# Attention values made for 256 pixels of each half in one job, with the column of ones in the weights

## The chip, the cores and the metric

The kernel runs on one core of a Trainium2 chip. The core has four compute engines, each with its own in-order queue: TensorE (PE in the profile, with its weight loads as PEld), VectorE (DVE), ScalarE (ACT) and GpSimd (POOL). SyncE (SP) issues most of the DMAs. Matrix products land in PSUM, everything else lives in SBUF. The metric is the device time of one execution in microseconds (us).

## The reference

The input `x` has 8 images of 192 channels and 64 x 64 pixels. Two layers follow each other, each with a residual sum and with a group normalisation `_gn` in front (32 groups of 6 channels). Cut to what matters:

```python
q = prelu(conv1x1(x, w1, b1), a1)        # 24 channels
k = prelu(conv1x1(x, w2, b2), a2)        # 24 channels
v = prelu(conv1x1(x, wa, ba), aa)        # 192 channels
score = softmax(einsum('bnc,bcm->bnm', q, k), axis=2)   # 4096 x 4096 per image
out = einsum('bnm,bmc->bnc', score, v)
...
x = x + attention(_gn(x))                # layer 0
x = x + density(_gn(x))                  # layer 1
```

The density layer sends every pixel minus and plus 0.5 through a small network for each channel (widths 1, 3, 3, 3, 1, with tanh gates) and takes the difference of two sigmoids.

## The kernel before

The 192 channels are three groups `g` of 64 partitions, and the 4096 pixels of an image are two halves `s` of 2048, so that 128 partitions hold 64 channels of either half. Everything is float32; each matrix product appears in the profile as two records.

**The stream.** Attention is a loop of 1024 steps: 8 images, 8 blocks of 512 query pixels (`NB`), 16 steps each (`STEPS`). A step puts on TensorE, in this order: the scores of the next step (`scores`, L786, 2 products into the PSUM tile `sc`), a row-maximum product for a block to come (`max_products`, L714, 2 products into `mx`, which VectorE reduces in L722), and the sums of this step (`attend`, L801, 8 products of 193 columns into one of the two tiles `turns`, named `b` in the profile). ScalarE takes the exponential of the scores (L790). The 193rd column of a values tile is 1, so the sums also give the softmax's denominator. `sc` and `mx` have one buffer each: the next scores wait for the exponential, and the next maximum product for the reduce.

**Jobs.** Whatever else needs PSUM while the stream runs is a job, which is a guest in the tile of `turns` that the running block doesn't use: keys and queries (`keys`, L626), values (`values`, L675), transposes of the maxima (L751) and of the output (L834), norms (L462, L477) and weights (L553, L558). `start_job` starts at most one per step, by rank, and only if enough PSUM halves are free and, where the job asks for `cols` of scratch, a scratch pair is. A job returns its parts as `(steps later, function, VectorE cost, ScalarE cost, TensorE credit)`. `run_due` adds the credit to what VectorE and ScalarE may spend on density work (`density_step`): units of small instructions, above all L1053 on VectorE, L1021, L1030, L1036 and L1046 on ScalarE. The whole order is thus written out when the kernel is built, step by step; the engines then run it in their queues' order.

**A values job** makes 128 pixels of both halves: 4 products (three channel groups and one with `one_row`, which adds the bias row) for each of two halves, the halves in the two tiles of 64 rows of the array, side by side. Then `prelu` evacuates: two relus on ScalarE (L602) from PSUM into a scratch pair, of x and of -x, and a merge on VectorE (L605) into the values tile. There are two scratch pairs, `pra` and `prb`, of 2 x 192 columns; `ready` says from which step each is free. A pair of 256-pixel input tiles `xi` thus needs two values jobs. The columns of ones are set once, by GpSimd (L590).

**The head.** The first image's keys and values and the maxima of its first blocks are made before the stream. There a loop takes one values job per turn from a list and one or two maximum products from another, into the tiles `sc_head` and `mx_head`, each reduced by L722. Values of the other seven images are made in the stream, during the image before.

**The tail.** After the last step, the density work that is left follows, with some of its sums on TensorE (L994).

`weights` scales the convolution weights by the norm for each image (`wa_sb` becomes `wf["v"]`) and makes the offset of the bias row (`wf["ba"]`, from `ba_row` and L558).

Of the kernel before, what the change touches and what calls it, by code (L numbers as in the profile page):

```python
# [9 lines left out]
F32 = mybir.dt.float32  # L10
AF = mybir.ActivationFunctionType
ALU = mybir.AluOpType
# [5 lines left out]
def kernel(  # L18
# [142 lines left out]
    for i in range(2):  # L161
# [3 lines left out]
        bb.append(w)  # L165
        w = const.tile([128, 1], F32, name=f"slope{i}")
        slope.append(w)
    wa_sb = const.tile([128, 3, C], F32, name="wa_sb")
    ba_row = const.tile([128, C], F32, name="ba_row")
    one_row = const.tile([128, 128], F32, name="one_row")  # L170
    vslope = const.tile([128, 1], F32, name="vslope")
    nslope = const.tile([128, 3], F32, name="nslope")
    for t in (*wr, ba_row, one_row):
        nc.vector.memset(t, 0.0)
    nc.vector.memset(one_row[0:1], 1.0)
    nc.vector.memset(one_row[R : R + 1], 1.0)

    for i in range(2):
        nc.vector.tensor_reduce(
# [24 lines left out]
    def spread():  # L204

        for i in range(2):
            for k in range(4):
                at = slice(32 * k, 32 * k + CR)
                p = slice(R * (k % 2), R * (k % 2) + R)
                nc.gpsimd.tensor_copy(wr[i][p, :, at], (s2 if k // 2 == i else s1)[p])  # L210
        for g in range(3):
            nc.gpsimd.tensor_copy(
                wa_sb[:, g, :].rearrange("p (h r) -> p h r", h=3),
                sa[:, g, :].rearrange("p (r h) -> p h r", h=3),
            )
        for s in range(2):
            p = slice(R * s, R * s + 1)
            nc.gpsimd.tensor_copy(
                ba_row[p].rearrange("p (h r) -> p h r", h=3),
                sb[p].rearrange("p (r h) -> p h r", h=3),  # L220
            )

# [131 lines left out]
    ]  # L354

    scratch = []
    for k in "ab":
        pair = []
        for i in range(2):
            u = work.tile([128, 2 * C], F32, tag=f"pr{k}{i}", name=f"pr{k}{i}")  # L360
            pair.append(u)
        scratch.append(pair)
    ready = [0, 0]


# [14 lines left out]
    def start_job(t):  # L380
        p = t % STEPS
        for n, (rank, make, hold, banks, cols) in enumerate(jobs):
            if stream[0] and (p < 3 or p + max(hold, 1) >= STEPS):
                continue
            rooms = [(pm, g) for pm, g in homes if sum(k <= t for k in g) >= banks]
            if not rooms:
                if rank < 2:
                    return
                continue
            k = [i for i in (1, 0) if ready[i] <= t and scratch[i][0].shape[1] >= cols]  # L390
            if cols and not k:
                continue
            del jobs[n]
            pm, guest = min(rooms, key=lambda r: max(r[1]))
            at_ = [i for i in range(2) if guest[i] <= t]
            for i in at_[:banks]:
                guest[i] = t + hold + 1
            if cols:
                ready[k[0]] = t + 2
            spot[0] = next(n for n, k in enumerate(turns + others) if k is pm), at_[0]  # L400
            parts = make(pm if banks == 2 else pm[:, at_[0], :], scratch[k[0]] if cols else None)
            for i, fn, cost, act, pe in parts:
                at(t + i, fn, cost, act, pe)
            return
# [130 lines left out]
    def weights(b, then):  # L535
# [26 lines left out]

        def offsets():
            pf = cell["pf"]
            for i in range(2):
                d = wf["b", i, b] = fold.tile([128, 2], F32, tag=f"b{i}", name=f"b{i}_{b}")
                cell["read"](nc.vector.tensor_tensor(
                    d[:, 0:1], bb[i], pf[:, 2 * i : 2 * i + 1], ALU.subtract
                ))
                nc.vector.tensor_scalar(d[:, 1:2], d[:, 0:1], -1.0, None, ALU.mult)  # L570
            d = wf["ba", b] = fold.tile([128, C], F32, tag="ba", name=f"ba_{b}")
            cell["read"](nc.vector.tensor_tensor(d, ba_row, pf[:, 4 : 4 + C], ALU.subtract))
            then()

        at(now[0] + 1, scale, 0.3, 2.0)
# [11 lines left out]
    vtiles = []  # L587
    for i in range(NC + 2):
        v = vpool.tile([128, 2, 4, C + 1], F32, tag=f"v{i}", name=f"v{i}")
        nc.gpsimd.memset(v[:, :, :, C : C + 1], 1.0)  # L590
        vtiles.append(v)
    qt = {}

# [66 lines left out]
            )  # L660
        made.add(("q", b, c))

    def values(b, d, k, what, done):

        t = xi[what, b, d]
        c, h = divmod(d, 2)

        def make(pv, u):
            if (b, c) not in vt:
                vt[b, c] = vtiles.pop(0)  # L670
            v = vt[b, c][:, :, 2 * h + k, 0:C]
            for g in range(4):
                for s in range(2):
                    p = slice(R * s, R * s + R)
                    nc.tensor.matmul(  # L675
                        pv[:, s, 0:C],
                        lhsT=t[p, g, k * 128 : k * 128 + 128] if g < 3 else one_row[p],
                        rhs=wf["v", b][p, g, :] if g < 3 else wf["ba", b][p],
                        start=g == 0, stop=g == 3,
                    )  # L680
            done()
            first, last = prelu(
                ("v", b, d, k), v, pv[:, :, 0:C], None, nslope[:, 2:3],
                [x[:, 0 : 2 * C].rearrange("p (s n) -> p s n", s=2) for x in u],
            )
# [106 lines left out]
    def attend(t):  # L792
# [5 lines left out]
        assert ("v", b, 2 * ORDER[p // 4] + p % 4 // 2, p % 2) in made  # L798
        for s in range(2):
            for j in range(4):  # L800
                nc.tensor.matmul(  # L801
# [496 lines left out]

    def use(b, d, what, t, k, v, after=0):

        left = [k + 2 * v]

        def done():
            left[0] -= 1
# [7 lines left out]
        def work():  # L1312
            if k:
                keys(b, d, what, done)
            if v:
                for i in range(2):
                    values(b, d, i, what, done)

        at(t, lambda: request("xi", begin))

# [63 lines left out]
    ahead.extend([place(m)[1:]] for m in range(STEPS, LEAD))  # L1384
    while todo or ahead:
        if todo:
            make, d, *k = todo.pop(0)
            make(0, d, *k, "first", lambda: None)
# [88 lines left out]
```

## Time and profile before

| What | Value |
|---|---|
| Median of 3 runs | 4778.19 us (4777.09 to 4778.64) |
| Profiled execution | 4772.86 us |
| Its span | 4771.1 us |
| PE busy | 4654.9 us, 98% |
| DVE busy | 4162.7 us, 87% |
| ACT busy | 3198.0 us, 67% |
| POOL busy | 865.9 us, 18% |
| L801 PE, sums of the stream, x16384 | 2955.0 us |
| L675 PE, values from `xi`, x1344, and the bias row, x512 | 139.5 us and 62.9 us |
| L602 ACT, relus of 384 columns, x144 and x112 | 62.5 us and 48.6 us |
| L605 DVE, merges of 384 columns, x72 and x56 | 43.9 us and 34.5 us |

Busy time is the union of an engine's instructions, and its share is an average over head, stream and tail. Products are pipelined, so the distance between two starts says more than a duration. In lines of the timeline the columns are the start, the time until the last of the merged instructions ends (both in us), the engine, the line of the kernel, the operation, output and inputs, shapes, the count, and in brackets the idle time before and what ended it. In lines by stretch, the columns are the stretch, its length, then busy time and instruction count of PE, PEld, DVE, ACT and POOL, the granted TensorE clock, the DMA share and GB/s.

### The profile page before, as it was taken

The page shows a single profiled execution, that of the slowest core. Times are in us where ns is not written, and L with a number is a line of the kernel's source. Part 1 is how long each engine was busy: PE and PEld are TensorE (multiplying, and loading weights), DVE is VectorE, ACT ScalarE, POOL GpSimd, SP SyncE. Part 2 cuts the span into 40 slices and gives each one's busy share as a digit, 9 for nine tenths or more (in the row PEclk, how much of TensorE's full clock was granted, in tenths as well). Part 3 has the DMA queues.
Part 4 walks back from the last instruction along what each step waited for, and adds up shares of the span by engine and source line. Part 5 has one row for each costly group of instructions (what it writes and reads, how often), then busy time and mean ns, then how long its engine had stood idle before and what let it go on. Part 6 is the DMA issues. An engine that isn't in the chain of part 4 may idle for free.

```text
span 4771.1 us, 69026 instructions
## 1 busy us (share of the span) xinstructions
PE 4654.9 (98%) x28432; PEld 3442.5 (72%) x28432; DVE 4162.7 (87%) x4289; ACT 3198.0 (67%) x3665; POOL 865.9 (18%) x842
## 2 busy tenths in 40 slices
PE   7999999999999999999999999999999999999796
PEld 5777777777777777777777777777777777777332
DVE  5433359999999999999999999999999999998888
ACT  2332246767677777876777767777777777778675
POOL 0000001222222212221312322132222122132000
PEclk9999999999999999999999999999999999999898
DMA  2101020111100111110110111101111101000000
GB/s 59 41 18 29 18 48 14 35 28 30 46 24 25 37 39 34 27 41 12 36 46 26 30 40 36 32 16 36 36 38 33 31 16 27 10 6 22 9 14 14
DMA packets 109328, 138.60 MB, mean 29 GB/s; under 512 B 17106, under 2 KB 82132, under 8 KB 109012
## 3 DMA queue, kind: packets, MB, share of 16 engines
q1 hardware_dynamic: 107776, 133.81, 11.5%
q8 instruction: 223, 3.65, 0.3%
q14 instruction: 93, 0.76, 0.1%
q10 hardware_dynamic: 1236, 0.37, 0.0%
HBM read 100.58 MB, written 29.36 MB: 27 GB/s over the span
## 4 chain that ended last, share of the span: by engine, by line
PE 95%; ACT 2%; DVE 2%; DMA 0%; issue 0%; POOL 0%; ACTq 0%; SPq 0%; DVEq 0%; POOLq 0%
PE b L801 60%; PE sc L786 22%; PE b L675 4%; PE b L994 2%; PE b L626 2%; PE mx L714 1%; PE sc_tail L994 1%; PE mx_tail L994 1%; DVE d L1053 1%; PE b L834 1%; PE b L751 1%; ACT d L1046 0%; ACT d L1021 0%; ACT e L790 0%; ACT d L1002 0%
## 5 line engine op out<-in xcount | busy, mean ns | idle before, releaser
L801 PEld LDWEIGHTS b<-v,e 128*128 128x128 f32 x16384 | 2651.1, 190 | 776.0 <-issue 764.6
L801 PE MATMUL b<-v,e 128*128 128x193 f32 x16384 | 2955.0, 334 | 0.0
L790 ACT ACTIVATE e<-sc 128x1024 f32<-128x1024 f32 x1024 | 1045.4, 1021 | 1320.1 <-PE mx L714 1282.6
L722 DVE TENSOR_REDUCE rm<-mx 128x1 f32<-128x1024 f32 x1002 | 1223.0, 1221 | 477.5 <-PE mx L714 471.1
L786 PE MATMUL sc<-q,k 25*128 25x512 f32 x4096 | 1154.2, 640 | 4.1 <-ACT e L790 3.8
L714 PE MATMUL mx<-k,q 24*128 24x512 f32 x4008 | 1129.4, 640 | 0.0
L1053 DVE SCALAR_TENSOR_TENSOR d<-d,lc,d 128x1024 f32<-128x1024 f32 x756 | 974.0, 1298 | 16.7 <-ACT d L1030 4.8
L1053 DVE SCALAR_TENSOR_TENSOR d<-d,wsp,d 128x1024 f32<-128x1024 f32 x684 | 876.2, 1284 | 50.6 <-ACT d L1046 42.5
L1174 POOL MEMSET pause<- 128x1 f32 x408 | 40.3, 99 | 3590.1 <-DVE d L1053 3590.1
L1053 DVE SCALAR_TENSOR_TENSOR d<-d,tf,d 128x1024 f32<-128x1024 f32 x540 | 685.7, 1287 | 0.4 <-ACT d L1036 0.4
L1036 ACT ACTIVATE d<-d 128x1024 f32<-128x1024 f32 x540 | 566.8, 1052 | 34.4 <-DVE d L1053 34.1
L786 PEld LDWEIGHTS sc<-q,k 25*128 25x128 f32 x4096 | 306.2, 183 | 229.6 <-issue 188.9
L1046 ACT ACTIVATE d<-d,cb,wsp 128x1024 f32<-128x1024 f32 x348 | 429.2, 1235 | 0.6
L1021 ACT ACTIVATE d<-xc,bn,wn 128x1024 f32<-128x1024 f32 x288 | 353.4, 1234 | 0.8 <-issue 0.8
L1084 POOL TENSOR_TENSOR d<-d,d 128x512 f32<-128x512 f32 x168 | 335.8, 1999 | 36.9 <-ACT d L1078 35.7
L1030 ACT ACTIVATE d<-xc,bn,wn 128x1024 f32<-128x1024 f32 x252 | 311.3, 1235 | 0.0
L714 PEld LDWEIGHTS mx<-k,q 24*128 24x128 f32 x4008 | 299.6, 183 | 9.1 <-DVE rm L722 8.2
L1209 POOL TENSOR_TENSOR d<-d,d 128x512 f32<-128x512 f32 x80 | 170.2, 2127 | 0.0
L1221 POOL TENSOR_TENSOR d<-d,d 128x512 f32<-128x512 f32 x80 | 170.1, 2126 | 0.5 <-issue 0.5
L1229 POOL TENSOR_TENSOR d<-d,d 128x512 f32<-128x512 f32 x80 | 159.4, 1992 | 1.7
L675 PE MATMUL b<-wv,xi 64*128 64x192 f32 x1344 | 139.5, 340 | 0.0
L675 PEld LDWEIGHTS b<-wv,xi 64*128 64x128 f32 x1344 | 106.5, 186 | 25.4 <-issue 23.6
(155 smaller groups left out, 2309.1 us busy)
## 6 DMA issues: line engine op xcount, KB each, us to landing
xi<-in_x_dram SPq DMA_DIRECT2D x280, 192.0 KB, 3.7
xc<-in_x_dram SPq DMA_DIRECT2D x64, 384.0 KB, 7.0
out_dram<-xc SPq DMA_DIRECT2D x94, 256.0 KB, 3.2
q<-qd SPq DMA_DIRECT2D x128, 128.0 KB, 2.7
k<-kq SPq DMA_DIRECT2D x64, 64.0 KB, 1.9
qd<-kq SPq DMA_DIRECT2D x64, 64.0 KB, 2.1
d<-in_x_dram SPq DMA_DIRECT2D x16, 192.0 KB, 4.1
out_dram<-xc SPq DMA_DIRECT2D x4, 128.0 KB
```

Of the source, the lines that this page charges most:

```text
L675: nc.tensor.matmul(pv[:, s, 0:C], lhsT=t[p, g, k * 128 : k * 128 + 128] if g < 3 else one_row[p], rhs=wf["v", b][p, g, :] if g < 3 else wf ...
L714: nc.tensor.matmul(sc[:, s, :], lhsT=tile_of(qt[b, n // 2], n, j)[r], rhs=kt[b][r, u : u + F], start=True, stop=True,)
L722: nc.vector.tensor_reduce(out=rowmax[b, n][:, j, k : k + 1], in_=sc, axis=AX.XY, op=ALU.max)
L786: nc.tensor.matmul(sc[:, s, :], lhsT=kt[b][r, k : k + 128], rhs=qt[b, n // 2][r, :, u : u + 256], start=True, stop=True,)
L790: return lambda: nc.scalar.activation(e, sc, AF.Exp)
L801: nc.tensor.matmul(a[:, j, 0 : C + 1], lhsT=e[:, s, j * 128 : j * 128 + 128], rhs=v[:, s, p % 4, :], start=p == 0 and s == 0 and j % 2 == ...
L1021: nc.scalar.activation(self.buf[k], self.src(), AF.Tanh, bias=bn[:, s, g, 0, i : i + 1], scale=wn[:, g, 0, i : i + 1],)
L1030: nc.scalar.activation(self.buf[k], self.src(), AF.Identity, bias=bn[:, s, g, 1, i : i + 1], scale=wn[:, g, 1, i : i + 1],)
L1036: nc.scalar.activation(self.buf[k], self.buf["l", k[1], k[2]], AF.Tanh)
L1046: nc.scalar.activation(self.buf[k], self.buf["l", n - 1, 0], AF.Identity, bias=offset, scale=wsp[:, g, w : w + 1],)
L1053: nc.vector.scalar_tensor_tensor(dst, src, factor, dst, ALU.mult, ALU.add)
L1084: return nc.gpsimd.tensor_tensor(z[:, n], z[:, n], dst[:, n], ALU.add)
```

## The change

One values job now makes 256 pixels of each half: both groups of 128 pixels, one after the other, into columns 0 to 192 and 193 to 385 of the same two PSUM banks. The evacuation is two relus of 772 columns and one merge of 772. Its scratch is both pairs together, which are now one pair of tiles of 772 columns; keys use one half of it, as before. Such a job starts only when both halves are free, and holds both for two steps. Its parts carry a credit of 2.75 for TensorE, 1.9 for ScalarE and 0.95 for VectorE, where each of the two jobs had 1.4, 1.1 and 0.62. The weights get a 193rd column of zeros and the bias row a 193rd element of one, so that the products give the column of ones, and the GpSimd memsets of it go away.

```diff
-    wa_sb = const.tile([128, 3, C], F32, name="wa_sb")
-    ba_row = const.tile([128, C], F32, name="ba_row")
+    wa_sb = const.tile([128, 3, C + 1], F32, name="wa_sb")
+    ba_row = const.tile([128, C + 1], F32, name="ba_row")
...
+    nc.vector.memset(wa_sb[:, :, C : C + 1], 0.0)
+    for k in (0, R):
+        nc.vector.memset(one_row[k : k + 1], 1.0)
+        nc.vector.memset(ba_row[k : k + 1, C : C + 1], 1.0)
...
-    for k in "ab":
-        pair = []
-        for i in range(2):
-            u = work.tile([128, 2 * C], F32, tag=f"pr{k}{i}", name=f"pr{k}{i}")
-            pair.append(u)
-        scratch.append(pair)
+    for i in range(2):
+        u = work.tile([128, 4 * C + 4], F32, tag=f"pr{i}", name=f"pr{i}")
+        scratch.append(u)
...
-            k = [i for i in (1, 0) if ready[i] <= t and scratch[i][0].shape[1] >= cols]
-            if cols and not k:
+            k = [i for i in (1, 0) if ready[i] <= t]
+            wide = cols > 2 * C
+            if cols and len(k) < 1 + wide:
                 continue
...
-            if cols:
+            u = None
+            if wide:
+                ready[:] = t + 2, t + 2
+                u = scratch
+            elif cols:
                 ready[k[0]] = t + 2
+                u = [x[:, 2 * C * k[0] : 2 * C * (k[0] + 1)] for x in scratch]
...
-                    pf[:, 4 : 4 + C], lhsT=cell["mb"][p], rhs=wf["v", b][p, g, :],
+                    pf[:, 4 : 5 + C], lhsT=cell["mb"][p], rhs=wf["v", b][p, g, :],
...
-        nc.gpsimd.memset(v[:, :, :, C : C + 1], 1.0)
...
-            v = vt[b, c][:, :, 2 * h + k, 0:C]
-            for g in range(4):
-                for s in range(2):
-                    p = slice(R * s, R * s + R)
-                    nc.tensor.matmul(
-                        pv[:, s, 0:C],
-                        ...
+            v = vt[b, c][:, :, 2 * h : 2 * h + 2, :].rearrange("p s k n -> p s (k n)")
+            for k in range(2):
+                for g in range(4):
+                    for s in range(2):
+                        p = slice(R * s, R * s + R)
+                        nc.tensor.matmul(
+                            pv[:, s, k * (C + 1) : (k + 1) * (C + 1)],
+                            ...
...
-                (0, lambda: None, 0.0, 0.0, 1.4), (1, first, 0.0, 1.1, 0.0),
-                (2, last, 0.62, 0.0, 0.0),
+                (0, lambda: None, 0.0, 0.0, 2.75), (1, first, 0.0, 1.9, 0.0),
+                (2, last, 0.95, 0.0, 0.0),
...
-        job(make, *((0, 1) if what == "v" else (k, 3)), 2, 2 * C)
+        job(make, *((0, 1) if what == "v" else (1, 3)), 2, 4 * C + 4)
...
-    todo += [(values, 2 * c + h, k) for c in ORDER for h in range(2) for k in range(2)]
+    todo += [(values, 2 * c + h) for c in ORDER for h in range(2)]
```

More of the change, by code (lines that the diff above doesn't have):

```diff
@@ L174 @@
         nc.vector.memset(t, 0.0)
-    nc.vector.memset(one_row[0:1], 1.0)
-    nc.vector.memset(one_row[R : R + 1], 1.0)
+    nc.vector.memset(wa_sb[:, :, C : C + 1], 0.0)
+    for k in (0, R):
+        nc.vector.memset(one_row[k : k + 1], 1.0)
+        nc.vector.memset(ba_row[k : k + 1, C : C + 1], 1.0)
     for i in range(2):
@@ L212, in spread @@
             nc.gpsimd.tensor_copy(
-                wa_sb[:, g, :].rearrange("p (h r) -> p h r", h=3),
+                wa_sb[:, g, 0:C].rearrange("p (h r) -> p h r", h=3),
                 sa[:, g, :].rearrange("p (r h) -> p h r", h=3),
@@ L218, in spread @@
             nc.gpsimd.tensor_copy(
-                ba_row[p].rearrange("p (h r) -> p h r", h=3),
+                ba_row[p, 0:C].rearrange("p (h r) -> p h r", h=3),
                 sb[p].rearrange("p (r h) -> p h r", h=3),
@@ L397, in start_job @@
                 guest[i] = t + hold + 1
-            if cols:
+            u = None
[3 more added lines that the diff above has]
+            elif cols:
                 ready[k[0]] = t + 2
+                u = [x[:, 2 * C * k[0] : 2 * C * (k[0] + 1)] for x in scratch]
             spot[0] = next(n for n, k in enumerate(turns + others) if k is pm), at_[0]
-            parts = make(pm if banks == 2 else pm[:, at_[0], :], scratch[k[0]] if cols else None)
+            parts = make(pm if banks == 2 else pm[:, at_[0], :], u)
             for i, fn, cost, act, pe in parts:
@@ L570, in offsets @@
                 nc.vector.tensor_scalar(d[:, 1:2], d[:, 0:1], -1.0, None, ALU.mult)
-            d = wf["ba", b] = fold.tile([128, C], F32, tag="ba", name=f"ba_{b}")
-            cell["read"](nc.vector.tensor_tensor(d, ba_row, pf[:, 4 : 4 + C], ALU.subtract))
+            d = wf["ba", b] = fold.tile([128, C + 1], F32, tag="ba", name=f"ba_{b}")
+            cell["read"](nc.vector.tensor_tensor(d, ba_row, pf[:, 4 : 5 + C], ALU.subtract))
             then()
@@ L661, in queries, with values @@
         made.add(("q", b, c))
-    def values(b, d, k, what, done):
+    def values(b, d, what, done):
         t = xi[what, b, d]
@@ L670, in make @@
                 vt[b, c] = vtiles.pop(0)
-            v = vt[b, c][:, :, 2 * h + k, 0:C]
-            for g in range(4):
-                for s in range(2):
-                    p = slice(R * s, R * s + R)
-                    nc.tensor.matmul(
-                        pv[:, s, 0:C],
[L677 to L680, printed above, removed]
+            v = vt[b, c][:, :, 2 * h : 2 * h + 2, :].rearrange("p s k n -> p s (k n)")
[5 more added lines that the diff above has]
+                            pv[:, s, k * (C + 1) : (k + 1) * (C + 1)],
+                            lhsT=t[p, g, k * 128 : k * 128 + 128] if g < 3 else one_row[p],
+                            rhs=wf["v", b][p, g, :] if g < 3 else wf["ba", b][p],
+                            start=g == 0, stop=g == 3,
+                        )
             done()
             first, last = prelu(
-                ("v", b, d, k), v, pv[:, :, 0:C], None, nslope[:, 2:3],
-                [x[:, 0 : 2 * C].rearrange("p (s n) -> p s n", s=2) for x in u],
+                ("v", b, d), v, pv[:, :, 0 : 2 * C + 2], None, nslope[:, 2:3],
+                [x.rearrange("p (s n) -> p s n", s=2) for x in u],
             )
             return [
-                (0, lambda: None, 0.0, 0.0, 1.4), (1, first, 0.0, 1.1, 0.0),
-                (2, last, 0.62, 0.0, 0.0),
+                (0, lambda: None, 0.0, 0.0, 2.75), (1, first, 0.0, 1.9, 0.0),
+                (2, last, 0.95, 0.0, 0.0),
             ]
-        job(make, *((0, 1) if what == "v" else (k, 3)), 2, 2 * C)
+        job(make, *((0, 1) if what == "v" else (1, 3)), 2, 4 * C + 4)
     rowmax = {}
@@ L797, in attend @@
         v = vt[b, ORDER[p // 4]]
-        assert ("v", b, 2 * ORDER[p // 4] + p % 4 // 2, p % 2) in made
+        assert ("v", b, 2 * ORDER[p // 4] + p % 4 // 2) in made
         for s in range(2):
@@ L1299, in use @@
     def use(b, d, what, t, k, v, after=0):
-        left = [k + 2 * v]
+        left = [k + v]
         def done():
@@ L1315, in work @@
             if v:
-                for i in range(2):
-                    values(b, d, i, what, done)
+                values(b, d, what, done)
         at(t, lambda: request("xi", begin))
@@ L1386 @@
         if todo:
-            make, d, *k = todo.pop(0)
-            make(0, d, *k, "first", lambda: None)
+            make, d = todo.pop(0)
+            make(0, d, "first", lambda: None)
         pair = list(zip(others, ahead.popleft() if ahead else ()))
```

## The prediction

> **What bounds the kernel now.** The first view read is the page: engine shares, then the chain that ended last.
>
> ```profile
> span 4771.1 us, 69026 instructions
> PE 4654.9 (98%) x28432; PEld 3442.5 (72%) x28432; DVE 4162.7 (87%) x4289; ACT 3198.0 (67%) x3665; POOL 865.9 (18%) x842
> PE 95%; ACT 2%; DVE 2%; DMA 0%; issue 0%; POOL 0%; ACTq 0%; SPq 0%; DVEq 0%; POOLq 0%
> ```
>
> TensorE is busy nearly always, and the chain runs through it for 95% of the span. An average hides stages, so the second view is busy time by stretch: head, stream, tail.
>
> ```profile
> 45.00:95.00 50.00, 46.37 (x363) 28.30 (x364) 37.12 (x45) 17.52 (x37) 0.00 (x0) 1.00 0.20 47
> 95.00:4420.00 4325.00, 4323.17 (x27383) 3280.49 (x27381) 3813.61 (x3913) 2939.92 (x3383) 849.93 (x805) 1.00 0.12 29
> 4420.00:4771.00 351.00, 266.38 (x620) 117.59 (x618) 295.10 (x275) 231.40 (x227) 10.66 (x11) 0.90 0.05 12
> ```
>
> In the stream (1024 steps from 94 to 4420 us) TensorE leaves 2 us of 4325 idle, VectorE is busy for 88% and ScalarE for 68%. There, time is what TensorE's queue holds. In the head and the tail it is not alone. The third view is TensorE's timeline over three steps.
>
> ```profile
> 603.30 0.70 PE L786 MATMUL sc<-q,k 25*128 25x512 f32 x2
> 604.38 2.88 PE L801 MATMUL b<-v,e 128*128 128x193 f32 x16
> 607.19 1.25 PE L675 MATMUL b<-wv,xi 64*128 64x192 f32 x12
> 608.26 0.49 PE L675 MATMUL b<-ba,one_row 64*128 64x192 f32 x4
> 608.69 0.70 PE L786 MATMUL sc<-q,k 25*128 25x512 f32 x2
> ```
>
> A values job stands alone between an attention block and the next scores and takes 608.69 - 607.19 = 1.50 us. Over the whole timeline, 693 plain steps have a median of 3.882 us and the 112 steps with a values job one of 5.382, none more than 1 ns from it: the job is paid in full, and none of it is hidden. The fourth view is the same timeline at the end of the head.
>
> ```profile
> 87.12 1.25 PE L675 MATMUL b<-wv,d 64*128 64x192 f32 x12
> 88.20 0.49 PE L675 MATMUL b<-ba,one_row 64*128 64x192 f32 x4
> 88.53 1.14 PE L675 MATMUL b<-wv,d 64*128 64x192 f32 x12
> 89.50 0.49 PE L675 MATMUL b<-ba,one_row 64*128 64x192 f32 x4
> 89.92 1.13 PE L786 MATMUL sc<-q,k 25*128 25x512 f32 x4
> 93.30 0.70 PE L786 MATMUL sc<-q,k 25*128 25x512 f32 x2 [2.25 <-ACT e L790]
> ```
>
> Two values jobs back to back take 89.92 - 87.12 = 2.80 us, not 3.00: going from the full array to two halves of 64 rows and back costs about 0.2 us, and here it is paid once for two jobs.
>
> **The stream: one change of array shape less per pair.** A wide job holds the same 32 TensorE records (16 products) as two narrow ones. By the rows it costs 2.80 us plus one column in 192 (0.5% of 2 x 1.30 us, 0.013): 2.81. Instead of 2 x 1.50 that is 0.187 less. Seven images make their values in the stream, 8 wide jobs each, and the built program has all 56 in steps of their own: 56 x 0.187 = **-10.5 us**.
>
> **ScalarE and VectorE.** Start to start, a relu of 384 columns takes 0.371 us on ScalarE and an exponential of 1024 takes 0.921, so one of 772 lies near 0.704; two replace four: 1.41 for 1.48 us. The merge on VectorE takes 0.526 at 384 columns, and L1053 takes 1.196 at 1024, so 772 lie near 0.93, for 1.05. Over 64 pairs that is 5 us of ScalarE and 8 us of VectorE, both with idle time in the stream: worth nothing directly. Cover gone, it would be 8 us. The Trainium skill (Perfetto Trace Analysis, Optimizing Scalar/DVE Operations) gives about 60 ns of overhead per VectorE operation; by that figure alone 64 merges fewer would be an estimated 4 us. The same section says that where these engines aren't saturated but cause bubbles on others, breaking instructions up may finish work sooner, which speaks against this change; by that rule the bubbles of the next part should grow.
>
> **The head: the order changes.** A wide job needs both scratch halves, so it may start only every second turn of the head's loop; narrow jobs alternated. In the built program's order a round of row maxima (one tile in `sc_head`, one in `mx_head`) formerly had a values job behind nearly every round. Now rounds stand in pairs with nothing between: R1 R2 W R3 R4 W R5 W R6 R7 W R8, transposes, S9 W S10 S11 W S12 S13 W S14 W, then the first scores (R round, S single tile, W wide job). A second tile in the same PSUM tile must wait for the reduce of the first:
>
> ```profile
> 46.55 1.22 DVE L722 TENSOR_REDUCE rm<-sc_head 128x1 f32<-128x1024 f32 x1
> 47.69 1.22 DVE L722 TENSOR_REDUCE rm<-mx_head 128x1 f32<-128x1024 f32 x1
> 48.82 0.48 DVE L605 SCALAR_TENSOR_TENSOR kq<-prb,nslope,prb 128x256 f32<-128x256 f32 x1
> ```
>
> Reduces follow each other by 1.14 us; a tile's matmuls came 1.27 after the start of the reduce they waited for (47.69 to 48.96); a reduce starts 1.18 after its matmuls (59.28 to 60.46); a tile alone takes TensorE 1.06, a round side by side 1.07. So two rounds in a row take 1.18 + 1.14 + 1.27 + 1.06 = 4.65 us, where two rounds with cover take 2.14; two single tiles 1.18 + 1.27 + 1.06 = 3.51. R8 to S9 takes 2.31 (second reduce) + 1.14 + 0.52 (72.19 to 72.71) + 0.56 (transposes) + 1.06 = 5.59. R2 ends 2.33 after 47.69, at 50.02. From there: 8 W x 2.81 = 22.48, two double rounds 9.30, R5 1.07, R8 to S9 5.59, two double singles 7.02, S14 1.06: 46.52. The first scores start at 96.54, not 89.92: **+6.6**. Behind them ScalarE evacuates the last job before it loads the table for the exponential: two relus of 0.81 and 0.70 instead of 0.49 and 0.37, so about **+0.6**. The scratch is single now, but each relu finds the merge before it done, except the last (0.1). Bounds for the head: +4, if half the lost cover is filled, and +9.
>
> **Stalls in the stream.** Plain steps exceed their median by 29.1 us in all, 5.0 of it in three steps (94, 1846 and 3488 us) in whose stretches the granted clock is 0.76. The other 24 come nearly all when a reduce or an exponential is late, about 2.4 of it per image in steps 12 to 17, where norm work and new density units meet. The planner gives a wide job 2.75 of credit at once and moves VectorE's density work by steps. I summed VectorE's work between each reduce and the next in both programs' order (rows' start-to-start times), against the step on TensorE with 1.6 us of grace for the reduce: surplus 7.3 us before, 8.6 after, all but 0.7 of it in steps 15 to 17 and near the end of the last image. So +1.3; the ledger sees only 7.3 of the 24, and scaled up it would be +4.3. I take **+2**, between -4 and +5.
>
> **Tail, start and stores.** TensorE's order in the tail is the same. On VectorE one L1053 (1.2 us), which ran at 4430.78 while L1250 waited for ScalarE, now stands behind L1251, ahead of the last residual and statistics that the final norm waits for: **+1.2** (-2 to +4, since the units after it are also reordered). Three small memsets more on VectorE (about 0.2 us) lie under its 9.4 us wait for x; six on GpSimd are gone from a stretch where it waits for weights; the 193rd column of the folded weights and bias costs some ns eight times. Nothing.
>
> **Sum.** -10.5 + 7.2 + 2 + 1.2 = -0.1. The profiled execution took 4772.86 us (span 4771.1 and 1.8 around it), 5.3 less than the median of the runs, 4778.19; the difference is applied to the latter: 4778.1, say 4778.
>
> **The rivals.** *Faster*: the head's pairs of rounds are covered better than I worked out (+4) and the stalls shrink by 4, since ScalarE and VectorE have 13 us less to do: -10.5 + 4 - 4 + 1.2 = -9.3, and with a tail unharmed -10.5: about 4768. For it: the steps are paid to the nanosecond. Against: the order of the head is fixed and its tiles do wait. *Slower*: the late reduce. The merge of 0.93 us in one piece stands ahead of reduces, and the credit of 2.75 lets three L1053 (3.6 us) stand beside it; 1.14 + 0.93 + 3.6 = 5.7 against 3.88 + 1.6 = 5.5. At 0.2 us for each of 56 jobs this costs 11: 4789. It decides once such a pile-up meets most of the jobs; the ledger finds it at few. *No saving inside the wide job*: the second half pays again, because it starts a new accumulation in the same bank: +10.4, 4788. Against it: the back-to-back row, though there the second job writes another tile.
>
> **Numbers.** No change (within 0.2%, 9.6 us, about what a measurement of this kernel can tell from no change): 0.62, own range 4769 to 4787. Faster 0.18. Slower 0.20, of which 0.12 for the late reduce and 0.08 for no saving. The range 4767 to 4790 takes in both other cases' centres and leaves out their far halves.
>
> **What would show it.** Right: a values step of 3.88 + 2.81 = 6.69 us; first attention block near 101.6, not 94.4 us; the stream from there some 8 us shorter; the tail about a microsecond longer. Wrong: a values step of 6.88; the first block before 98 us; excess of plain steps over 40 or under 15 us.

## The result, and the profile after

The changed kernel takes 4796.05 us (median of 5 runs, 4792.53 to 4797.34) against 4777.09 us for the one before (4772.67 to 4778.64): a ratio of 1.0044, with an interval of [1.0033, 1.0055]. It is slower by 0.4%, and outside the predicted range, which ended at 4790. The profiled execution after took 4796.05 us, with a span of 4794.3 us, 23.2 us longer than before (the medians are 19.0 apart; the execution profiled before was 4.2 us under its median). First the page, its lines for the span, the busy time and the chain that ended last (the changed kernel's lines are numbered 6 higher where it matters: values L681, maxima L720 and L728, scores L792, exponential L796, sums L807, density merge L1059):

```profile
span 4794.3 us, 68761 instructions
PE 4657.6 (97%) x28432; PEld 3452.8 (72%) x28432; DVE 4155.3 (87%) x4228; ACT 3192.3 (67%) x3537; POOL 857.1 (18%) x836
PE 91%; DVE 4%; ACT 3%; issue 1%; POOL 0%; DMA 0%; SPq 0%; ACTq 0%; DVEq 0%; POOLq 0%
```

VectorE and ScalarE have a little less to do, as worked out (7.4 and 5.7 us). But the chain now leaves TensorE for 9% of the span instead of 5%, and TensorE is busy 2.7 us longer for the same number of products. The busy time by stretch (head, stream, tail) says where:

```profile
45.00:114.00 69.00, 57.20 (x368) 36.69 (x366) 35.85 (x36) 16.13 (x22) 0.00 (x0) 0.83 0.17 39
114.00:4438.00 4324.00, 4315.55 (x27386) 3282.51 (x27384) 3804.92 (x3857) 2936.55 (x3271) 840.60 (x805) 1.00 0.12 29
4438.00:4794.00 356.00, 267.14 (x622) 118.34 (x618) 297.73 (x275) 231.30 (x227) 11.45 (x11) 0.90 0.05 12
```

The head ends at 114 us, not 94, and its granted clock is 0.83 where it was 1.00. The stream idles for 8.5 us of TensorE where it idled for 2. The tail is 5 us longer. From TensorE's timeline, to the first and from the last attention block:

| us, profiled execution | before | after | difference | predicted |
|---|---|---|---|---|
| first product (22.2 to 24.1 in the 14 executions below) | 22.85 | 24.07 | +1.2 | 0 |
| from there to the first attention block | 71.5 | 90.0 | +18.5 | +7.2 |
| stream, 112 or 56 values jobs | 168.0 | 158.0 | -10.0 | -10.5 |
| stream, what plain steps exceed 3.882 by, and small rests | 29.1 | 37.7 | +8.6 | +2 |
| tail | 350.8 | 355.7 | +4.9 | +1.2 |

The row of the jobs is 112 x 1.500 and 56 x 2.822: the median of the steps with a job, 5.382 and 6.704, less 3.882. One of them in TensorE's timeline, in image 4:

```profile
2537.07 2.88 PE L807 MATMUL b<-v,e 128*128 128x193 f32 x16
2539.88 1.25 PE L681 MATMUL b<-wv,xi 64*128 64x193 f32 x12
...
2542.70 0.70 PE L792 MATMUL sc<-q,k 25*128 25x512 f32 x2
```

A wide job takes 2542.70 - 2539.88 = 2.82 us, as predicted (2.81). So the job does what it should; the loss lies in the head and in the stalls. The head's timeline, first the products that waited:

```profile
49.44 1.13 PE L720 MATMUL sc_head<-k,q 24*128 24x512 f32 x4 [0.61 <-DVE rm L728]
...
58.57 1.48 PE L720 MATMUL sc_head<-k,q 24*128 24x512 f32 x4 [1.31 <-DVE rm L728]
...
72.99 1.13 PE L720 MATMUL sc_head<-k,q 24*128 24x512 f32 x4 [1.31 <-DVE rm L728]
...
82.10 0.63 PE L757 MATMUL b<-ident,negmax 128*128 128x128 f32 x4 [2.96 <-DVE negmax L751]
...
92.25 1.13 PE L720 MATMUL sc_head<-k,q 24*128 24x512 f32 x4 [1.33 <-DVE rm L728]
...
100.26 1.13 PE L720 MATMUL sc_head<-k,q 24*128 24x512 f32 x4 [1.33 <-DVE rm L728]
...
112.04 1.22 PE L792 MATMUL sc<-q,k 25*128 25x512 f32 x2 [2.90 <-ACT e L796]
```

The brackets are the idle time: 8.85 us before the six products of the maxima and transposes, where the kernel before had 0.25 and 1.07, and 2.90 before the second scores, where it had 2.25. The kernel before:

```profile
50.34 1.25 PE L675 MATMUL b<-wv,d 64*128 64x192 f32 x12 [0.25 <-ACT prb L602]
...
72.71 0.63 PE L751 MATMUL b<-ident,negmax 128*128 128x128 f32 x4 [1.07 <-DVE negmax L745]
```

That is 8.2 us more of waits; less 8 x 0.18 for the wide jobs, the order cost 6.7, against 7.2 predicted. The other 11.8 us of the head have another cause. Two wide jobs of this head, and a pair of rounds, from the timeline after:

```profile
61.71 2.30 PE L681 MATMUL b<-wv,d 64*128 64x193 f32 x12
...
66.64 0.70 PE L720 MATMUL sc_head<-k,q 24*128 24x512 f32 x2
...
70.53 0.70 PE L720 MATMUL sc_head<-k,q 24*128 24x512 f32 x2
...
75.18 1.25 PE L681 MATMUL b<-wv,d 64*128 64x193 f32 x12
...
97.80 1.13 PE L720 MATMUL sc_head<-k,q 24*128 24x512 f32 x4
...
101.31 1.25 PE L681 MATMUL b<-wv,d 64*128 64x193 f32 x12
...
104.14 1.13 PE L720 MATMUL sc_head<-k,q 24*128 24x512 f32 x4
```

The job from 61.71 takes 4.93 us, the one from 101.31 takes 2.83, for the same products. From 59.2 to 66.0 us the granted clock is 0.50, from 101.3 to 104.2 it is 1.00. Where it is full, the other pieces also came as worked out: the two rounds from 70.53 take 4.65 us, the two single tiles from 97.80 take 3.51. The trace has five stretches of half clock that begin in this head, from 52.4, 59.2, 83.1, 93.4 and 110.4 us, of 3.4 or 6.8 us, 27.2 us in all, of which 24.1 lie before the first attention block; the kernel before has none there. The eight wide jobs take 30.65 us instead of 8 x 2.81 = 22.48.

### The profile page after: what moved, and what is told of

Its sections match the earlier page's. It is cut to its first block, busy times and chain, and to the rows that moved or that the text cites. A ratio compares the mean times of both kernels' runs of the same rounds, so it can differ in the third digit from the quotient of the medians.

```text
span 4794.3 us, 68761 instructions
## 1 busy us (share of the span) xinstructions
PE 4657.6 (97%) x28432; PEld 3452.8 (72%) x28432; DVE 4155.3 (87%) x4228; ACT 3192.3 (67%) x3537; POOL 857.1 (18%) x836
## 4 chain that ended last, share of the span: by engine, by line
PE 91%; DVE 4%; ACT 3%; issue 1%; POOL 0%; DMA 0%; SPq 0%; ACTq 0%; DVEq 0%; POOLq 0%
PE b L807 57%; PE sc L792 21%; PE b L681 4%; DVE d L1059 3%; PE b L1000 2%; PE b L631 2%; PE mx L720 1%; PE mx_tail L1000 1%; PE sc_tail L1000 1%; PE b L840 1%; ACT d L1052 1%; PE b L757 1%; ACT d L1027 1%; ACT e L796 1%; DVE rm L728 1%
## 5 line engine op out<-in xcount | busy, mean ns | idle before, releaser
L807 PEld LDWEIGHTS b<-v,e 128*128 128x128 f32 x16384 | 2651.1, 190 | 776.7 <-issue 770.6
L807 PE MATMUL b<-v,e 128*128 128x193 f32 x16384 | 2954.9, 334 | 0.0
L796 ACT ACTIVATE e<-sc 128x1024 f32<-128x1024 f32 x1024 | 1044.7, 1020 | 1312.4 <-PE mx L720 1269.6
L728 DVE TENSOR_REDUCE rm<-mx 128x1 f32<-128x1024 f32 x1002 | 1223.7, 1221 | 485.6 <-PE mx L720 475.9
L792 PE MATMUL sc<-q,k 25*128 25x512 f32 x4096 | 1155.1, 640 | 11.3 <-ACT e L796 11.0
L720 PE MATMUL mx<-k,q 24*128 24x512 f32 x4008 | 1130.3, 640 | 0.0
L1059 DVE SCALAR_TENSOR_TENSOR d<-d,lc,d 128x1024 f32<-128x1024 f32 x756 | 971.6, 1295 | 16.5 <-ACT d L1036 4.8
L1059 DVE SCALAR_TENSOR_TENSOR d<-d,wsp,d 128x1024 f32<-128x1024 f32 x684 | 879.4, 1288 | 52.6 <-ACT d L1052 44.7
L1059 DVE SCALAR_TENSOR_TENSOR d<-d,tf,d 128x1024 f32<-128x1024 f32 x540 | 688.0, 1296 | 0.4 <-ACT d L1042 0.4
L1180 POOL MEMSET pause<- 128x1 f32 x408 | 39.9, 98 | 3603.4 <-DVE d L1059 3603.4
L792 PEld LDWEIGHTS sc<-q,k 25*128 25x128 f32 x4096 | 306.4, 183 | 237.9 <-issue 182.1
L720 PEld LDWEIGHTS mx<-k,q 24*128 24x128 f32 x4008 | 299.9, 183 | 11.1 <-DVE rm L728 10.1
L681 PE MATMUL b<-wv,xi 64*128 64x193 f32 x1344 | 134.7, 332 | 0.0
L607 ACT ACTIVATE pr<-b 128x772 f32<-128x772 f32 x128 | 97.0, 814 | 48.3 <-PE b L681 45.4
```

Of the source, the lines that this page charges most:

```text
L681: nc.tensor.matmul(pv[:, s, k * (C + 1) : (k + 1) * (C + 1)], lhsT=t[p, g, k * 128 : k * 128 + 128] if g < 3 else one_row[p], rhs=wf["v", ...
L720: nc.tensor.matmul(sc[:, s, :], lhsT=tile_of(qt[b, n // 2], n, j)[r], rhs=kt[b][r, u : u + F], start=True, stop=True,)
L728: nc.vector.tensor_reduce(out=rowmax[b, n][:, j, k : k + 1], in_=sc, axis=AX.XY, op=ALU.max)
L792: nc.tensor.matmul(sc[:, s, :], lhsT=kt[b][r, k : k + 128], rhs=qt[b, n // 2][r, :, u : u + 256], start=True, stop=True,)
L796: return lambda: nc.scalar.activation(e, sc, AF.Exp)
L807: nc.tensor.matmul(a[:, j, 0 : C + 1], lhsT=e[:, s, j * 128 : j * 128 + 128], rhs=v[:, s, p % 4, :], start=p == 0 and s == 0 and j % 2 == ...
```

## The experiments

Theories, after the result: the head is the order's idle time plus the half clock that the idle time brings; in the stream either the large pieces (two relus and a merge of 772 columns) hold up exponentials and reduces, or the credit, given once for two jobs, moves density work into full steps. What came out, with the profiled execution's head (first product to first attention block), half clock in it, stream and tail, the excess of the plain steps, and that excess without the steps that half clock touches:

| Kernel | median us (runs) | ratio to before | head | half clock | stream | excess | without half clock | tail |
| --- | --- | --- | --- | --- | --- | --- | --- | --- |
| before | (see above) | 1 | 71.5 | 0 | 4325.9 | 29.1 | 24.2 | 350.8 |
| after | 4796.05 (5) | 1.0044 [1.0033, 1.0055] | 90.0 | 24.1 | 4324.5 | 37.7 | 32.9 | 355.7 |
| narrow_head | 4779.64 (10) | 1.0013 [1.0003, 1.0023] | 74.0 | 5.5 | 4328.1 | 40.5 | 34.1 | 354.6 |
| narrow_stream | 4792.58 (5) | 1.0036 [1.0023, 1.0049] | 89.4 | 23.9 | 4327.1 | 29.2 | 24.2 | 347.9 |
| filled | 4786.18 (10) | 1.0024 [1.0015, 1.0034] | 83.2 | 9.6 | 4324.9 | 37.4 | 32.9 | 354.3 |
| credit | 4801.20 (4) | 1.0056 [1.0041, 1.0071] | 89.0 | 20.5 | 4327.8 | 40.1 | 34.4 | 360.0 |
| narrow_c1 | 4767.23 (1) | one run | 71.2 | 0.1 | 4320.9 | 23.4 | 19.3 | 350.5 |
| narrow_c2 | 4770.65 (1) | one run | 71.9 | 1.1 | 4325.2 | 27.7 | 22.4 | 348.0 |
| wide_c2 | 4780.14 (10) | 1.0008 [0.9999, 1.0018] | 72.1 | 1.3 | 4327.9 | 39.9 | 31.9 | 354.6 |
| split | 4783.44 (1) | one run | 72.2 | 1.7 | 4329.6 | 40.7 | 35.7 | 355.9 |
| spread | 4771.12 (10) | 0.9992 [0.9983, 1.0002] | 71.7 | 0 | 4321.8 | 35.0 | 31.6 | 350.0 |
| spread_c1 | 4765.56 (10) | 0.9982 [0.9973, 0.9992] | 72.2 | 2.4 | 4318.9 | 32.1 | 28.2 | 350.4 |
| narrow_c1_timed | 4770.62 (10) | 0.9992 [0.9983, 1.0002] | 74.3 | 5.2 | 4323.3 | 25.2 | 19.3 | 350.1 |
| narrow_lump | 4795.46 (1) | one run | 71.4 | 0 | 4350.3 | 52.0 | 44.0 | 348.0 |

The kernel before had a median of 4774.06 beside the first four experiments, 4775.30 beside the next four and 4774.02 beside the last four. "Loss" below is what steps of a typical one of the images 3 to 6 (images and steps counted from 0) run over their median, counting those over 60 ns and without half-clock steps: 3.9 us per image before, 6.1 after. Of the edits only the lines that matter are shown.

### The two halves of the change, apart

**narrow_head**: the head makes its values in narrow jobs, in the order of before; the stream is that of after.

```diff
-    def values(b, d, what, done):
+    def values(b, d, what, done, ks=(0, 1)):
...
-    todo += [(values, 2 * c + h) for c in ORDER for h in range(2)]
+    todo += [(values, 2 * c + h, (k,)) for c in ORDER for h in range(2) for k in range(2)]
```

> The head makes the first image's values in 16 narrow jobs as the kernel before did; the stream keeps the 56 wide jobs of the changed kernel, in the same order of instructions. Theory 'head': the changed kernel lost some 18 us because pairs of maximum rounds stand uncovered in the head and TensorE, idle between them, was granted half its clock; here the first attention block starts at 94 to 96 us instead of 114, the granted clock in the head is 1.0, and the total is 4778 to 4783 us. Theory 'late reduce': the loss lies in the stream, where a wide evacuation delays the reduces; here the head gains at most 7 us (its order alone) and the total stays above 4788 us. Either way the stream from the first to the last attention block should take 4324.5 us as in the changed kernel.

**narrow_stream**: the reverse; the stream makes narrow jobs, each with 1.4, 1.1 and 0.62, and its order is that of before.

```diff
-                values(b, d, what, done)
+                for i in range(2):
+                    values(b, d, what, done, (i,))
```

> The other half alone: 8 wide jobs in the head, 112 narrow jobs in the stream, whose order of instructions is that of the kernel before. Theory 'head': the first attention block starts at 112 to 115 us with stretches of half clock, the stream takes 4326 us as before, and the total is 4793 to 4798 us. Theory 'late reduce': the total is below 4786 us, since the stream no longer holds a wide job.

With the narrow head the head is back at 74.0 us and the time at 1.0013; with the narrow stream the excess is back at 29.2 and the tail at 347.9, but the head stays at 89.4 and the time at 1.0036. So the head carries most of the loss, and the stalls and the longer tail come with the wide jobs of the stream. Theory 'head' holds, with small misses: narrow_head's clock was 0.95 and its first attention block came at 96.5 us, narrow_stream's at 111.6. Narrow_head's stream was 3.6 us longer than after's although the order is the same: the steps that half clock touches cost 7.2 us in it and 4.9 in after, and two late reduces of image 5 (steps 36 and 38), 1.2 together, are not in after's execution.

### The clock in the head

**filled**: after, with 38 products of 126 columns that nobody reads, put ahead of the waiting products (2, 6, 6, 12, 6 and 6).

```diff
+    def busy(n):
+        for _ in range(n):
+            nc.tensor.matmul(
+                pm[:, 0, 386:512], lhsT=ident, rhs=ident[:, 0:126], start=True, stop=True
+            )
...
+        if pair and lone[0]:
+            busy(2 if pair[0][1] == (0, 1, 0) else 6)
```

> The changed kernel with its order, but in the six places of the head where TensorE waited for a reduce or for the transposes' input, products of 126 columns of the identity are put in front of the waiting product (2, 6, 6, 12, 6 and 6 of them, each about 0.22 us at full clock), into PSUM columns that nothing reads. They do no useful work and should end before the wait does. Theory 'idle halves the clock': the granted clock stays near 1.0 in the head, every wide job takes 2.8 us there instead of up to 5.4, the first attention block starts at 102 to 104 us instead of 114, and the total is 4784 to 4788 us. Theory 'load halves the clock' (the half clock follows the dense 64-row products, not the gaps): the clock still falls, the first block starts at 114 us or later, and the total is 4796 us or more.

The heads by stretch, of filled and of narrow_head (after's line stands above):

```profile
45.00:105.00 60.00, 56.70 (x432) 38.61 (x432) 35.85 (x36) 15.29 (x20) 0.00 (x0) 0.92 0.16 38
```

```profile
45.00:96.00 51.00, 47.42 (x360) 29.08 (x356) 36.69 (x44) 17.05 (x36) 0.00 (x0) 0.95 0.18 45
```

With more work in it the head is 6.8 us shorter, and its half clock went from 24.1 to 9.6 us. Each product of a filler takes the place of idle time, so what was gained is the clock's. The expectation of a clock near 1.00 was a miss: two stretches of 6.8 us stayed, one of them from 102.7 us, in the 2.90 us of waiting for the first exponential, which were not filled; what keeps the other, from 48.1, is open. The first attention block came at 105.5 us, not 102 to 104. The table prices the half clock: take half of it off each head, and the four with wide jobs in the head (after, narrow_stream, filled, credit) are left with 77.4 to 78.8 us, the ten others with 71.0 to 71.7. So a microsecond of half clock in the head costs about half of one, and the order about 7, as the waits gave.

### Credit or large pieces

**credit**: after, with larger costs for the wide job.

```diff
-                (0, lambda: None, 0.0, 0.0, 2.75), (1, first, 0.0, 1.9, 0.0),
-                (2, last, 0.95, 0.0, 0.0),
+                (0, lambda: None, 0.0, 0.0, 2.8), (1, first, 0.0, 2.2, 0.0),
+                (2, last, 1.24, 0.0, 0.0),
```

> The changed kernel with other numbers for the planner alone: a wide job carries 2.8 of credit for TensorE, 2.2 for ScalarE and 1.24 for VectorE, the sums of two narrow jobs, in place of 2.75, 1.9 and 0.95. No instruction is added or taken away; where density work stands in the stream changes. Theory 'chance placement': the excess of plain steps over their median (37.7 us in the changed kernel, 29.1 before) moves by 2 to 8 us in either direction though every wide job still costs 2.82 us. Theory 'wide pieces': it stays within 1.5 us of 37.7, since what delays the reduces are the wide relus and merges themselves. The head stays at 114 us, total 4788 to 4804 us.

The excess went up by 2.4, not down, without the half clock by 1.5, and the stream and the tail grew by 3.3 and 4.2. That is too small to decide between the two theories. The stalls did move: in image 4 those of steps 52 and 68 are gone, and steps 66 and 77 have some of 0.87 and 0.60 us. Larger costs are no cure.

**narrow_c1** and **narrow_c2**: before, with other costs per narrow job (1.375, 0.95, 0.475, which is half of the wide job's, and 1.5, 1.1, 0.62). **wide_c2**: narrow_head with 2.82, 1.45 and 1.0 for the wide job.

> The kernel before with other numbers for the planner alone: each of its narrow values jobs carries 1.375 of credit for TensorE, 0.95 for ScalarE and 0.475 for VectorE, half of a wide job's, in place of 1.4, 1.1 and 0.62. No wide piece exists in it. In images 3 to 6 the kernel before loses 3.9 us per image in late reduces and exponentials, the changed kernel 6.1; their tails (from the last attention block) take 351 and 356 us. Theory 'placement': the loss depends on where the planner's bookkeeping happens to put density work, so here, with the same instructions as before, the loss per image moves by over 1 us (to below 3 or above 5) or the tail by over 2 us. Theory 'wide pieces': only the 772-column relus and merges make the extra loss, so it stays at 3.9 within 0.5 us and the tail at 348 to 351 us.

> As the run above, with 1.5 of credit for TensorE, 1.1 for ScalarE and 0.62 for VectorE per narrow job: a second draw of the planner's placement without any wide piece. 'Placement': loss per image and tail differ from both other kernels with narrow jobs by over 1 us and 2 us; 'wide pieces': 3.9 us per image and a tail of 348 to 351 us.

> Narrow jobs in the head, wide jobs in the stream, and the planner's numbers for a wide job set to what the trace of the changed kernel shows: 2.82 for TensorE, 1.45 for ScalarE, 1.0 for VectorE. Head as with narrow jobs (first block at 94 to 97 us). 'Placement': the loss per image may fall as well as rise against the 6.1 us of the changed kernel, by over 1 us; with luck the total is 4768 to 4775 us, below the kernel before. 'Wide pieces': the loss stays within 1 us of 6.1 per image, and the total is 4777 to 4784 us.

Costs alone move a narrow kernel by a few microseconds of excess (19.3, 22.4 and 24.2 without the half clock), and none brings it near after's 32.9; the wide kernel stays at 31.9 with costs near its real ones. The losses per image are 2.75, 3.1 to 3.7 and 6.2 us. So narrow_c1 moved as 'placement' expects, narrow_c2 in its tail but in its loss by less than it expects, and wide_c2 came out as 'wide pieces' expects, in loss and in time; the next run decides against that theory. Wide_c2's time, 1.0008, can't be told from before's or from narrow_head's.

**split**: narrow_head, but the wide job's evacuation is in halves again: four relus and two merges of 386 columns.

```diff
-            first, last = prelu(("v", b, d, ks), v, pv[:, :, 0 : len(ks) * (C + 1)], ...)
+            for j, k in enumerate(ks):
+                pairs.append(prelu(("v", b, d, (k,)), ..., pv[:, :, j * (C + 1) : (j + 1) * (C + 1)], ...))
```

> Narrow jobs in the head; in the stream the wide job keeps its 16 products in one row on TensorE and the planner's numbers of the changed kernel, so density work stands where it did, but the evacuation is in two halves: four relus and two merges of 386 columns. 'Wide pieces': the loss per image falls from 6.1 to about 3.9 us. 'Placement': it stays at 6.1 within 0.5 us, at the same steps of the image (18, 24, 52 and 68). A values step stays at 6.70 us.

The loss per image is 7.1 us, not less than after's 6.1 and above what either theory expects, and in the same steps (18, 24, 52, 68). The size of the pieces is not what stalls. Nor do the stalls stand at the wide jobs: those are in steps 44, 46, 56, 61, 115, 118, 120 and 124 of an image. ScalarE's and TensorE's timelines of after in step 24 of image 4 show one stall (0.79 us) behind a late exponential, and VectorE's and TensorE's in step 52 one (0.91 us) behind a late reduce:

```profile
2394.14 1.28 ACT L1219 ACT_TABLE_LOAD   x1
2395.44 1.15 ACT L1219 ACTIVATE d<-d 128x512 f32<-128x512 f32 x2
2396.49 0.61 ACT L1221 ACTIVATE d<-d 128x512 f32<-128x512 f32 x1
2397.01 1.00 ACT L796 ACTIVATE e<-sc 128x1024 f32<-128x1024 f32 x1
```

```profile
2398.07 0.70 PE L792 MATMUL sc<-q,k 25*128 25x512 f32 x2 [0.72 <-ACT e L796]
```

```profile
2516.79 2.60 DVE L1059 SCALAR_TENSOR_TENSOR d<-d,lc,d 128x1024 f32<-128x1024 f32 x2
2519.31 1.28 DVE L1059 SCALAR_TENSOR_TENSOR d<-d,tf,d 128x1024 f32<-128x1024 f32 x1
2520.50 1.22 DVE L728 TENSOR_REDUCE rm<-mx 128x1 f32<-128x1024 f32 x1
```

```profile
2521.77 1.13 PE L720 MATMUL mx<-k,q 24*128 24x512 f32 x4
```

In step 24 a table load and three pieces of density work stand ahead of the exponential, and the scores wait for it; in step 52 three density merges stand ahead of the reduce, and the next maximum product waits. No values job is near. The order that the planner wrote has put density work into steps that had no time to spare. In the whole of images 3 to 6, late exponentials cost 1.8 us per image where they cost 0.1 before, and late reduces 4.3 where they cost 3.8.

**narrow_lump**: before, except that the first narrow job of a pair carries the whole 2.75, 1.9 and 0.95, and the second nothing. No wide job, no large piece.

```diff
-                (0, lambda: None, 0.0, 0.0, 1.4), (1, first, 0.0, 1.1, 0.0),
-                (2, last, 0.62, 0.0, 0.0),
+                (0, lambda: None, 0.0, 0.0, 2.75 * (1 - k)), (1, first, 0.0, 1.9 * (1 - k), 0.0),
+                (2, last, 0.95 * (1 - k), 0.0, 0.0),
```

> The kernel before with 16 narrow jobs, of which the first of each pair carries the planner's numbers of a whole wide job (2.75, 1.9 and 0.95) and the second none. 'Lump': the loss per image rises from 3.9 to 5 to 7 us though no job is wide, above all in steps 18, 24, 52 and 68, and the stream grows to 4328 to 4340 us. 'Number of jobs': it stays below 4.5 us, with the steps of the kernel before (17, 22, 4, 12).

This is the sharpest of the runs. Its stream by stretch, and step 52 of image 4 in TensorE's timeline:

```profile
95.00:4445.00 4350.00, 4342.12 (x27388) 3288.86 (x27384) 3807.42 (x3913) 2939.72 (x3383) 840.27 (x805) 1.00 0.12 29
```

```profile
2511.19 0.70 PE L786 MATMUL sc<-q,k 25*128 25x512 f32 x2 [0.83 <-ACT e L790]
```

narrow_c1 has the same jobs and the same sum of costs, given half and half: stream 4320.9, excess 23.4 (19.3 without the half clock), loss 2.75 per image. Given as one lump: 4350.3, 52.0 (44.0) and 8.3. Both sizes are beyond the expectation. Steps 18 and 52, which stall in after, stall here too (0.96 and 0.90 us, step 52 behind an exponential instead of a reduce); 24 and 68 don't. The planner also sets the jobs themselves in other steps: the first eight of an image stand in 40, 41, 46, 53, 56, 57, 62 and 69, in narrow_c1 in 38, 39, 44, 45, 54, 55, 60 and 61. So a lump of credit alone makes such stalls, by the order that it makes the planner write; what part of them is density work moved and what part jobs moved was not told apart.

**spread** and **spread_c1**: narrow_head, with the wide job's credit given in two parts one step apart, as two narrow jobs would; 1.4, 1.1, 0.62 each, or 1.375, 0.95, 0.475.

```diff
-                (0, lambda: None, 0.0, 0.0, 2.75), (1, first, 0.0, 1.9, 0.0),
-                (2, last, 0.95, 0.0, 0.0),
-            ]
...
+                (0, lambda: None, 0.0, 0.0, 1.4), (1, first, 0.0, 1.1, 0.0),
+                (2, last, 0.62, 0.0, 0.0),
+            ] + [
+                (1, lambda: None, 0.0, 0.0, 1.4), (2, lambda: None, 0.0, 1.1, 0.0),
+                (3, lambda: None, 0.62, 0.0, 0.0),
+            ][: 3 * len(ks) - 3]
```

> Narrow jobs in the head, wide jobs in the stream, but the planner's numbers of a wide job are laid over the steps as two narrow jobs in a row would lay them: credit 1.4 at its step and 1.4 at the next, ScalarE 1.1 and 1.1, VectorE 0.62 and 0.62. The instructions of the job stay as they are. Theory 'lump': a credit of 2.75 in one step, of which the cap on the planner's credit lets some go, shifts density work to steps that are full, and the loss per image in images 3 to 6 (6.1 us with all three numbers tried for wide jobs, 2.8 to 3.9 with narrow jobs) falls to 2.5 to 4.5 us; stream 4314 to 4320 us instead of 4324.5, total 4763 to 4772 us. Theory 'number of jobs': with eight jobs per image instead of sixteen the other jobs find their places earlier, and that moves density work; the loss stays at 5.5 to 6.5 us and the total at 4776 to 4783 us.

> As the run above, with credit 1.375 and 1.375, ScalarE 0.95 and 0.95, VectorE 0.475 and 0.475: the numbers of the narrow kernel that lost 2.75 us per image. 'Lump': loss per image 2 to 4 us, total 4760 to 4770 us. 'Number of jobs': 5.5 to 6.5 us and 4776 to 4783 us.

**narrow_c1_timed** is narrow_c1, timed in rounds beside these.

> The kernel before with the planner's credit of 1.375, 0.95 and 0.475 per narrow job, timed beside the kernel before; its single time was 4767 us, its stream 5.0 us shorter than that of the kernel before (1.7 of it one half-clock stretch fewer). 'Placement' expects 4768 to 4773 us beside 4773 to 4777 for the kernel before, that is 0.05% to 0.15% faster without one instruction less; if the one time was chance in the half-clock stretches, it is within 2 us of the kernel before.

Spreading the credit took the stalls of steps 18, 24 and 68 away, and that of step 52 in spread_c1 (0.34 us stay in spread). The loss fell to 5.1 and 4.6 per image, between what 'lump' and 'number of jobs' expect; new stalls came, such as 0.63 us in step 117. The jobs moved too, the first four of an image from steps 44, 46, 56 and 61 to 39, 44, 53 and 57. The stream fell to 4321.8 and 4318.9, and the tail to 350. The stream stayed above the 4314 to 4320 expected of a full cure in the first, and 7 us of excess (9 without the half clock) above narrow_c1_timed in the second. So the lump is a part of the wide kernel's loss; the rest is open. spread_c1 beats both kernels: 4765.56 us (4762.84 to 4767.99), 0.9982 [0.9973, 0.9992], while narrow_c1_timed, with its costs and narrow jobs, can't be told from before. It is 5.1 us below narrow_c1_timed. The one run of the same program as narrow_c1, 4767.23, lies just under its ten here (4767.85 to 4773.26). Page and stream of spread_c1:

```profile
span 4765.5 us, 68821 instructions
PE 94%; ACT 3%; DVE 2%; DMA 0%; issue 0%; POOL 0%; SPq 0%; ACTq 0%; DVEq 0%; POOLq 0%
96.00:4415.00 4319.00, 4313.53 (x27388) 3281.84 (x27384) 3790.92 (x3857) 2934.70 (x3271) 862.82 (x805) 1.00 0.12 29
```

The chain is with TensorE for 94% again, and the stream is 7.0 us shorter than before's 4325.9: the 10 us of the jobs, of which 3 go to stalls.

## Why the prediction was wrong

**The stream's saving: right.** 10.0 us for 10.5, the wide job 2.822 us for 2.81. The rival "no saving inside the wide job", a step of 6.88, fell. The Trainium skill (TensorEngine Tiling (Array Packing), Key Properties) says that changing the tiling mode drains TensorE; the 0.18 us saved per pair fit that, though no run shows the drain by itself. The wide job's products have a column more than the narrow ones had: against narrow_stream, whose narrow jobs have 193 columns too and take 5.393 - 3.882 = 1.511 us, a wide job saves 0.20.

**The head: the order right, the clock missed.** The sum of +7.2 was right as far as it went: the waits give +6.7. The step that failed is "From there: 8 W x 2.81 = 22.48": the durations were taken from a head whose granted clock was 1.00, and the idle time that the same paragraph found was not asked what it would do to the clock, although the prediction itself had three stretches of the stream at a clock of 0.76. The eight jobs took 30.65, 8.2 us more, and rounds, transposes and first scores the rest of the 11.8, with 24.1 us of the head at half clock. Filled showed that 6.8 us of it go when the idle time is filled. The upper bound of +9 was 9.5 us short, more than the 6 us by which the time missed the range.

**The stalls: the ledger failed.** +2 was taken, with an upper bound of +5, and it was +8.6. The ledger counted VectorE's surplus against a reduce's grace in the order of both programs, and saw 1.3. It left ScalarE out: of the 2.2 us more per image, 1.7 are late exponentials, such as the one of step 24 behind a table load and tanh pieces, which no row of VectorE shows. It also missed late reduces: of its surplus all but 0.7 us stood in steps 15 to 17 and near the end of the last image, and step 52 alone waits 0.91 us in image 4. The rival "late reduce" named the credit of 2.75 and was right in part: as one lump it makes such stalls (narrow_lump), and spread out it takes some of them away; its merge in one piece is not it (split), and its place, at the jobs, is not either.

**The tail.** Its step was right: the last attention block to the first product of the final norm went from 20.37 to 21.54 us, the +1.2 of the one L1053 ahead of the last statistics. But the density sums behind it are late by 2.2 and then 2.95 us, and the end by 4.9, just beyond the bound of +4. Tails are 348 to 351 us in narrow_stream, spread and the narrow kernels and 354 to 360 with the lump in the wide ones. That it is which units the planner leaves to the tail is only argued: narrow_lump has a lump, and a tail of 348.0.

**Breaking up or joining.** Breaking up instructions where they cause bubbles was the rule of the Trainium skill weighed (Perfetto Trace Analysis, Optimizing Scalar/DVE Operations); the bubbles did grow. But in the head what was too coarse is a job of TensorE, with which the loop alternates, and in the stream breaking up the evacuation gained nothing (split).

**What it comes to.** 1.2 + 18.5 - 1.4 + 4.9 = +23.2 us in the profiled executions. None of the signs that the prediction listed as wrong came: the step was 6.70 and the excess stayed under 40. The first attention block was looked for on the early side, before 98 us, and came at 114. Of the signs of being right only the step came; the stream was 1.4 us shorter, not 8.

Open: what keeps a half clock in filled's head; what the remaining loss of the streams of spread and spread_c1 (5.1 and 4.6 us per image against 2.75 in narrow_c1) is due to; the tail.

## What to carry to other kernels

Merging small jobs of TensorE saves a change of array shape each time (0.18 us here, a column more included), and is worth it where TensorE's queue is the bound; where the small jobs were the cover between products that wait, keep them small, and price the lost cover with the clock too, not with the waits alone. When two jobs become one, look at what a planner was told about each: give the merged job's credit over as many steps as the two had, or the order written for the rest of the work changes, and stalls come in steps far away. And a ledger of one engine says nothing about stalls that another engine makes.

## What the runs showed of the hardware

Short gaps can halve the clock. None of the idle gaps shown above reached 3 us (0.61, 1.31, 1.31, 2.96, 1.33, 1.33, 2.90), and still 24.1 of 69 us ran at half clock. Not every gap does it: after those at 72.99 and 100.26 the clock stayed at 1.00 up to the next gap. The Trainium skill (TensorE: Matmul & The Clock Gate, HAM oscillation) has as its abstract rule that gaps over about 3.4 us are to be avoided; by that rule none of these would matter, and these runs differ from it. Its 3.4 us do show in another place: nearly every half-clock stretch in these traces lasts a multiple of them.

The half clock comes in the stream too, without a gap. In image 4 of narrow_lump the products of 2 columns that make the weights stand shortly before it; TensorE's timeline, and the stretch:

```profile
2399.61 1.40 PE L553 MATMUL b<-nrm,w 128*128 128x2 f32 x12
...
2403.29 4.41 PE L801 MATMUL b<-v,e 128*128 128x193 f32 x16
2407.63 0.70 PE L786 MATMUL sc<-q,k 25*128 25x512 f32 x2
```

```profile
2403.00:2406.40 3.40, 3.40 (x14) 3.11 (x11) 3.20 (x8) 1.97 (x2) 0.00 (x0) 0.50 0.00 0
```

TensorE is busy throughout and is granted 0.50, and the attention block takes 4.34 us to the next scores instead of 2.81. It comes in some images of some executions (6.8 us in all begin in the stream of after, 10.2 in before's, 17.0 in narrow_lump's, and 6.8 and 13.6 in two executions of one program, narrow_c1 and narrow_c1_timed), so that a profile taken once can differ by a few microseconds for this alone. That small products count as rest for the clock is a reading of this, not shown.
